# A graph attention layer: GpSimd's gathers spaced by an iota instead of waits for TensorE, and lookups issued ahead of kept-back products

## The chip, the cores and the metric

The kernel runs on one core of a Trainium2 chip. The metric is the device time of one execution in microseconds. Engines are named as the profile names them: PE is TensorE (its weight loads stand apart as PEld), DVE is VectorE, ACT is ScalarE, POOL is GpSimd and SP is SyncE.

## The reference

One layer of attention over the edges of a graph, with a residual and a layer norm. There are 12,500 nodes with 64 features, and 400,000 edges with 64 features, sorted by destination. Low-numbered nodes have by far the most edges.

```python
def _L0_gnn_ref(nfeats, efeats, W_ne, W_attn, b_attn, W_out, src, dst):
    h_src = nfeats[src]
    h_dst = nfeats[dst]
    z_att = jnp.concatenate([h_src, h_dst, efeats], axis=-1)
    e = jax.nn.leaky_relu(z_att @ W_attn + b_attn, negative_slope=0.01)[:, 0]
    m = jnp.concatenate([h_src, efeats], axis=-1) @ W_ne
    emax = jax.ops.segment_max(e, dst, num_segments=N)
    ex = jnp.exp(e - emax[dst])
    denom = jax.ops.segment_sum(ex, dst, num_segments=N)
    alpha = ex / denom[dst]
    z = jax.ops.segment_sum(alpha[:, None] * m, dst, num_segments=N)
    return jax.nn.relu(jnp.concatenate([nfeats, z], axis=-1) @ W_out)
x = _layernorm(x + _L0_gnn_ref(x, edge_attr_64, ...), axis=-1)
```

## The kernel before, in words

Edges are taken in 782 groups of 512 (128 partitions x 4). The groups go two ways.

**Gathered groups** (654 of them, from group 128 on) run in 42 chunks of mostly 16 groups, and a chunk in four tiles of four groups. For each group GpSimd issues four indirect DMAs (`gather`, L331). Each fetches one row of 65 numbers for each of 128 edges from a table in HBM into the tile `zx`, so a full chunk has 64 gathers. `zx` has eight buffers (`ZB`), two chunks' worth, and a buffer comes free when the products that read it are done. For a tile, VectorE makes the edges' scores (`scores`, L371 to L392) and, once the chunk's softmax is known, the weights `w` (L792). TensorE multiplies `zx` by `w` (`products`, L809, 16 matrix products a tile, each two matmul instructions in the profile), and VectorE adds the result into `acc` (L828).

**Dense groups** (the first 128, whose few destinations have very many edges) need no gather. TensorE looks up the sources' scores by a one-hot product (`look_turn` on ScalarE, `look_products` L442 on TensorE, `look_scores` L469 to L475 on VectorE). Later it counts, for each source node, the weights of its edges (`dense_counts`: one-hots `big` by ScalarE L483 and L484, weighted one-hots `lows` by VectorE L486, products L491, sum L509), and a product with all nodes' features (`node_products`, L568) ends each run of groups. Lookups run from chunk 1 on and counts from chunk 5 on, up to five groups in a chunk. They are woven into the chunks by hand.

**Order.** The engines' queues hold the program's order; nothing is reordered. A chunk issues the scores of its four tiles with pieces of dense work between them. After them comes the softmax, a chain of scans on VectorE with transposes of short rows on TensorE (L599 to a row, L602 back). It is cut into steps; after each of its first four parts `dense_work(n)`, n = 0 to 3, issues a piece of dense work. The products of a chunk's first two tiles (`NOW`) follow its softmax at once. Those of the third and fourth are kept back in `later`, and `some_products` issues them in the steps of the next chunk: a whole tile in step 0 and half a tile in the steps after it.

**The gathers' waits.** `BEHIND` lists places among a chunk's 64 gathers and for each a step of the chunk before: gather 28 waits for the last TensorE instruction issued in step 0, 33 for step 1, 42 for step 2, 48 for step 3, 56 and 61 for the products of the first and second tile. These waits hold from chunk 3 to the last of the full ones. `latest()` finds the instruction.

**In a step** the order is: lookup scores of the step before, sums, kept-back products, then the one-hot for a lookup (ScalarE, `look_turn`), the load of the row after it (SP, `look_row`), and the lookup's matmuls. The one-hot is made one lookup ahead.

Of the kernel before, what the change touches and what calls it, by code (L numbers as in the profile page):

```python
# [15 lines left out]
P = 128  # L16
# [9 lines left out]
S = 48  # L26
BG = 32
BIG = 6
LOWS = 6
SG = 4  # L30
BS = 16
DO = BS + 1
# [17 lines left out]
LATE = 8.0  # L50
NOW = 2
HALF = 2
BEHIND = ((28, 0), (33, 1), (42, 2), (48, 3), (56, "first"), (61, "second"))

BF16 = mybir.dt.bfloat16
I16 = mybir.dt.int16
# [3 lines left out]
def sorted_path(ctx, tc, x, dst, idx, edge, w_ne, w_attn, b_attn, w_out, out, flag):  # L60
# [6 lines left out]
    nc = tc.nc  # L67
# [11 lines left out]
    const = ctx.enter_context(tc.tile_pool(name="const", bufs=1))  # L79
# [33 lines left out]
    def nodes_of(g):  # L113
        return next(n for upto, n in NODS if g < upto)
# [7 lines left out]
    def kept_at(g):  # L122
        d = round_of(g)
        return g - begins[d] + d % 2 * BD
# [12 lines left out]
    for i in range(2):  # L137
# [20 lines left out]
    twice = const.tile([P, P], F32, name="twice")  # L158
    nc.vector.memset(twice, 0.0)

    low_rows = dram.tile([DG, P, T], BF16, name="low_rows")
    p_col = const.tile([P, 1], F32, name="p_col")
    nc.gpsimd.iota(p_col, pattern=[[0, 1]], base=0, channel_multiplier=-1,
                   allow_small_or_imprecise_dtypes=True)
    places = const.tile([P, NB * NOD], I16, name="places")
    nc.gpsimd.iota(places, pattern=[[1, NB * NOD]], base=0, channel_multiplier=0,
                   allow_small_or_imprecise_dtypes=True)
# [156 lines left out]
    def gather(g0, n, srcs, b0, plain, steps=()):  # L324

        zx = feats.tile([P, SG, T, EW + D], F32, name="zx")
        for g in range(n):
            for t in range(T):
                r = RP if g0 + g == NG - 1 else P
                at = srcs[0:r, g0 + g - b0, t:t + 1]  # L330
                row = nc.gpsimd.indirect_dma_start(  # L331
                    out=zx[0:r, g, t, 1:EW] if plain else zx[0:r, g, t, 0:EW], out_offset=None,
                    in_=x[:, :] if plain else table[:, :],
                    in_offset=bass.IndirectOffsetOnAxis(ap=at, axis=0))
                step = dict(BEHIND).get((g0 + g - b0) * T + t)
                if step is not None and step in steps:
                    tc.add_manual_dep(row.ins, steps[step].name,
                                      mybir.DependencyInfo(mybir.DependencyClass.Sync, mybir.DependencyReason.DATA),
                                      reason="gathers do not run ahead of the tensor engine")
        return zx  # L340
# [77 lines left out]
    def look_row(g):  # L418

        row = work.tile([P, P * T], BF16, name="low_of", bufs=1)  # L420
        nc.sync.dma_start(out=row, in_=low_rows[g:g + 1].rearrange("g p t -> g (p t)").to_broadcast([P, P * T]))
        return row

    def big():
        return work.tile([P, P, T], F32, name="big", bufs=BIG)

    def look_turn(row):

        hot = big()
        flat_ = hot.rearrange("l p t -> l (p t)")  # L430
        nc.scalar.activation(flat_, row, AF.Square, bias=p_col)
        nc.scalar.activation(flat_, flat_, AF.Relu, scale=-1.0, bias=1.0)
        return hot

    def spare():
        return psum.tile([P, SG, P], F32, name="pg", bufs=4).rearrange("p a b -> p (a b)")

    def look_products(hot, bank_):

        found = bank_[:, 0:T * NB].rearrange("p (t h) -> p t h", t=T)  # L440
        for t in range(T):
            nc.tensor.matmul(found[:, t, :], hot[:, :, t], s_src, start=True, stop=True)  # L442
        return found
# [33 lines left out]
    def dense_counts(g):  # L477
# [3 lines left out]
        for t in range(T):  # L481
            hi = big().rearrange("l p t -> l (p t)")[:, 0:wide]
            nc.scalar.activation(hi, places[:, 0:wide], AF.Square, bias=place[:, t, g:g + 1])  # L483
            nc.scalar.activation(hi, hi, AF.Relu, scale=-1.0, bias=1.0)  # L484
            lows.append(work.tile([P, P], F32, name="lows", bufs=LOWS))
            nc.vector.tensor_scalar(lows[t], count_, low[:, t, g:g + 1], kept[:, t, kept_at(g):kept_at(g) + 1],  # L486
# [15 lines left out]
    def dense_sum(g, to):  # L502

        _, vs = nc.values_load_multi_w_load_instructions(
            rel[0:1, g:g + 1], engines=(EngineType.DVE,), min_val=0, max_val=ND - nodes_of(g),
            skip_runtime_bounds_check_because=within)
        n = min(FIT, nodes_of(g))
        at = counts[:, :, ds(vs[0], n)]
        nc.vector.tensor_tensor(at, at, to.rearrange("p (h n) -> p h n", n=n), op=OP.add)  # L509
        for j in range(nodes_of(g) - FIT):  # L510
            at = counts[:, :, ds(vs[0] + FIT + j, 1)]
            nc.vector.tensor_tensor(at, at, more_nodes[j].unsqueeze(2), op=OP.add)
# [77 lines left out]
    def node_sum(g0, z):  # L590

        at = accd[0:D, ds(node_of(g0), ND)]
        nc.vector.tensor_tensor(at, at, z, op=OP.add)
# [222 lines left out]
    def add_in(g0, n, pg, b0, fac):  # L816
# [4 lines left out]
        for g in range(n):  # L821
            if g == 0 and fac is not None:
# [13 lines left out]
                   allow_small_or_imprecise_dtypes=True)  # L836
# [40 lines left out]
    with before:  # L877
# [23 lines left out]
        with tc.manual_schedule(engines={EngineType.DVE, EngineType.Pool, EngineType.Activation, EngineType.PE, EngineType.SP}):  # L901
# [30 lines left out]
            for g0 in range(0, NG, 3 * P):  # L932
                n = min(3 * P, NG - g0)
# [46 lines left out]
    def late_of(k):  # L980

        nc.vector.tensor_scalar(lates[:, k:k + 1], d0b[:, starts[k] + sizes[k] - 1:starts[k] + sizes[k]],
                                float(S - RING - zeroed[-1] * P), None, op0=OP.add)

    def raised():

        worst = tiny.tile([P, 4], F32, name="worst")
        bad = tiny.tile([P, 4], F32, name="bad")
        for i, (col, op) in enumerate(((fars, OP.max), (ups, OP.max), (lates, OP.max), (earlies, OP.min))):
            nc.vector.tensor_reduce(worst[:, i:i + 1], col, axis=AX.X, op=op)  # L990
        nc.vector.tensor_scalar(bad[:, 0:3], worst[:, 0:3], 0.0, None, op0=OP.is_gt)
        nc.vector.tensor_scalar(bad[:, 3:4], worst[:, 3:4], 0.0, None, op0=OP.is_lt)
        pbad = psum.tile([P, SG, P], F32, name="pg", bufs=4)[0:1, 0, 0:4]
        nc.tensor.matmul(pbad, ones_col, bad, start=True, stop=True)
        some = tiny.tile([1, 1], F32, name="some")
        nc.vector.tensor_reduce(some, pbad, axis=AX.X, op=OP.max)
        nc.vector.tensor_scalar(some, some, 1.0, None, op0=OP.min)
        nc.vector.tensor_copy(flag, some)
# [114 lines left out]
    with loop:  # L1113
# [9 lines left out]
        def add_up(most=SG * BG):  # L1123

            while sums and most:
                g0, n, pg, b0, fac = sums.pop(0)
                add_in(g0, n, pg, b0, fac)
                most -= 1
                k = starts.index(b0)
                if g0 + n == b0 + sizes[k]:  # L1130
                    done.extend(due[k])
# [16 lines left out]
        seen, dense_carry, resolved_at, at_rest = [], None, None, []  # L1148
# [3 lines left out]
        def alike(todo, ends_=chunk_ends):  # L1152
            n = 0
            while n < min(each_of(todo[0]) if todo else 0, len(todo)) and not (n and todo[n] in edges_) and not (n and todo[n] in ends_):
                n += 1
            return [todo.pop(0) for _ in range(n)]
# [12 lines left out]
        with tc.manual_schedule(engines={EngineType.PE, EngineType.DVE, EngineType.Activation, EngineType.SP, EngineType.Pool}):  # L1169
            ready, turns = {}, []  # L1170
            resting, batch_looks, batch_counts = None, [], []
# [12 lines left out]
            for k, G in enumerate(sizes):  # L1184
# [7 lines left out]
                if k:  # L1192
                    joined = resting
                    batch_looks = alike(looks, ())
# [16 lines left out]
                for i, (g0, n) in enumerate(lots[k]):  # L1211
# [5 lines left out]
                    if k and i == 0 and batch_looks:  # L1217
                        loads = look_loads(batch_looks[0], len(batch_looks))
                        rows_ahead = [look_row(batch_looks[0])]
# [90 lines left out]
                def dense_work(n):  # L1310

                    nonlocal opened, summed, resolved_at, node_z
                    if n == 1 and final:
                        late_of(k)
                        raised()
                    if n == 0 and node_z:
                        node_sum(*node_z)
                        if node_z[0] + chunk_sizes[-1] == DG:
                            resolved_at = k
                        opened = node_z = None  # L1320
                    if seen:
                        look_scores(*seen.pop(0))
                    if n > 1 and behind:
                        sums.append(behind.pop(0))
                    add_up(1)
                    if n in (0, 2, 3):
                        while open_counts:
                            dense_sum(*open_counts.pop(0))
                    for half in range(2 if n == 0 else 1):
                        if later:  # L1330
                            some_products()
                    if n + 1 < len(batch_looks):
                        if n:
                            turns.append(look_turn(rows_ahead.pop(0)))
                            if n + 2 < len(batch_looks):
                                rows_ahead.append(look_row(batch_looks[n + 2]))
                        seen.append((batch_looks[n + 1], look_products(turns.pop(0), spare())))
                    inner = batch_counts[len(early_counts):]
                    for g in inner[n - 4:][:1] if len(inner) >= 4 - n > 0 else ():
                        open_counts.append(dense_counts(g))  # L1340
# [511 lines left out]
```

## Time and profile before

| | |
|---|---|
| time, median of 3 runs | 4607.04 us (4581.74 to 4616.41) |
| the profiled execution's own time | 4585.0 us |
| its span, first to last instruction | 4583.3 us |
| mean granted TensorE clock | 0.675 |
| gathers | 2552 from the table, 64 from x |

The profile is that of one execution. A group of instructions is named by line, engine and operation, with output and inputs; `[idle before <-releaser]` gives the engine's idle time before an instruction and what ended it. "issue" means that the profile shows nothing that it waited for, and "remote" that a semaphore came at a time at which no instruction that adds to it ends. Ends of matmuls are modelled. The page's clock digits of the first fifth are 9 or 8 because the trace holds no clock record before 871 us.

### The profile page before, as it was taken

The numbers are of one execution on the slowest core, as the hardware profiler recorded it, in microseconds if no ns is written. First come the engines' busy times: TensorE is split into PE (matmuls) and PEld (weight loads), VectorE is DVE, ScalarE is ACT, GpSimd is POOL, SyncE is SP. The second block draws the span as 40 slices with busy tenths as digits, with TensorE's granted clock in tenths as the row PEclk, the third lists the DMA queues.
The fourth block names the chain that finished last, engine by engine and source line by source line (L and its number), as shares of the span: only waits on it lengthen the run. The fifth ranks groups of instructions, "written<-read, shape, count | busy, mean of one in ns | idle before, by whom it ended". The sixth has DMA issues, their size and how long they took to land. (4 is left out here: it accounts for less than half of the span.)

```text
span 4583.3 us, 38977 instructions
## 1 busy us (share of the span) xinstructions
PE 2480.8 (54%) x10315; PEld 2021.9 (44%) x10315; DVE 2158.0 (47%) x5618; ACT 1367.3 (30%) x2963; POOL 2478.9 (54%) x2644
## 2 busy tenths in 40 slices
PE   0144455565656667575666564455455565555544
PEld 0144445444545455454444444344343444444444
DVE  4444545454545545454535354444434454444346
ACT  0111223333323324242424232232323333323212
POOL 7566655555554555545464555555555545565543
PEclk9999999855556556566656566566566666666655
DMA  8222322232222222222222222222212222222111
GB/s 110 63 59 59 78 60 69 56 75 60 61 55 63 61 55 62 52 62 52 57 51 58 45 61 51 52 53 53 53 43 46 59 48 47 49 46 50 41 36 36
DMA packets 452951, 257.79 MB, mean 56 GB/s; under 512 B 266314, under 2 KB 410801, under 8 KB 452722
## 3 DMA queue, kind: packets, MB, share of 16 engines
q1 hardware_dynamic: 367036, 167.23, 14.4%
q0 software_dynamic: 83936, 87.27, 11.5%
q8 instruction: 88, 1.44, 0.1%
q14 instruction: 141, 1.16, 0.1%
q10 hardware_dynamic: 1750, 0.70, 0.1%
HBM read 248.17 MB, written 6.80 MB: 56 GB/s over the span
## 5 line engine op out<-in xcount | busy, mean ns | idle before, releaser
L331 POOL DMA_INDIRECT zx<-table,srcs x2552 | 2409.1, 944 | 2022.6 <-issue 823.1
L809 PE MATMUL pg<-w,zx 128*128 128x16 f32 (+9 forms) x5088 | 1063.0, 378 | 160.6 <-issue 118.1
L809 PEld LDWEIGHTS pg<-w,zx 128*128 128x128 f32 x5088 | 1047.8, 314 | 178.8 <-issue 118.9
L491 PE MATMUL pg<-big,lows 128*128 128x490 f32 (+3 forms) x1024 | 618.2, 758 | 733.3 <-DVE lows L486 256.0
L491 PEld LDWEIGHTS pg<-big,lows 128*128 128x128 f32 x1024 | 279.2, 293 | 1008.2 <-issue 731.1
L483 ACT ACTIVATE big<-places,place 128x490 f32<-128x490 int16 (+3 forms) x512 | 318.0, 621 | 581.5 <-remote 323.8
L442 PE MATMUL pg<-s_src,big 128*128 128x98 f32 x1024 | 282.0, 440 | 100.6 <-issue 100.6
L599 PE MATMUL lines<-ident,bnd 128*1 128x128 f32 x168 | 47.8, 384 | 500.4 <-ACT bnd L702 329.6
L442 PEld LDWEIGHTS pg<-s_src,big 128*128 128x128 f32 x1024 | 256.2, 328 | 101.7 <-issue 101.4
L471 DVE TENSOR_TENSOR pr<-pr,pg 128x392 f32<-128x392 f32 x128 | 72.0, 562 | 475.7 <-PE pg L442 283.8
L828 DVE TENSOR_TENSOR acc<-acc,pg 128x16 f32 (+9 forms) x654 | 121.7, 186 | 342.2 <-remote 235.1
L484 ACT ACTIVATE big<-big 128x490 f32<-128x490 f32 (+3 forms) x512 | 277.3, 542 | 16.3
L568 PE MATMUL pg<-xall,counts 128*128 128x256 f32 (+1 forms) x650 | 191.9, 447 | 120.9 <-issue 120.9
L599 PEld LDWEIGHTS lines<-ident,bnd 128*1 128x1 f32 x168 | 12.4, 96 | 522.3 <-ACT bnd L702 346.4
L486 DVE TENSOR_SCALAR lows<-fixed,low,kept 128x128 f32<-128x128 f32 x512 | 176.4, 403 | 105.9 <-remote 80.1
L376 DVE TENSOR_REDUCE soft<-pr 128x16 f32<-128x1024 f32 (+2 forms) x168 | 201.5, 1199 | 42.4 <-remote 24.4
L371 ACT ACTIVATE fixed<-wrow 128x144 f32<-128x144 f32 (+8 forms) x168 | 44.2, 263 | 593.8 <-DVE pr L469 171.3
L568 PEld LDWEIGHTS pg<-xall,counts 128*128 128x128 f32 (+1 forms) x650 | 146.5, 229 | 160.1 <-issue 137.4
L383 DVE TENSOR_TENSOR hot<-fixed,drel 128x576 bf16<-128x576 f32 (+8 forms) x168 | 106.8, 636 | 199.1 <-ACT fixed L371 183.9
L374 DVE TENSOR_TENSOR pr<-ze,lines 128x1024 f32<-128x1024 f32 (+2 forms) x168 | 198.6, 1182 | 2.1 <-DMA ze<-in_edge_dram 2.0
L509 DVE TENSOR_TENSOR counts<-counts,pg 128x490 f32 (+3 forms) x128 | 74.9, 585 | 250.5 <-remote 164.8
L372 ACT ACTIVATE zx<-ze 128x1024 f32<-128x1024 f32 (+2 forms) x168 | 174.0, 1036 | 5.6 <-issue 1.0
(308 smaller groups left out, 2743.9 us busy)
## 6 DMA issues: line engine op xcount, KB each, us to landing
ze<-in_edge_dram SPq DMA_DIRECT2D x157, 512.0 KB
zx<-table,srcs POOLq DMA_INDIRECT x2552
low_of<-low_rows SPq DMA_DIRECT2D x128, 128.0 KB
ep<-in_edge_dram SPq DMA_DIRECT2D x128, 128.0 KB
wrow<-wins SPq DMA_DIRECT2D x152, 96.0 KB
ed<-in_edge_dram SPq DMA_DIRECT2D x14, 640.0 KB
ed<-in_edge_dram SPq DMA_DIRECT2D x14, 384.0 KB
table<-xall SPq DMA_DIRECT2D x7, 455.0 KB
```

The source lines that it names most:

```text
L331: row = nc.gpsimd.indirect_dma_start(out=zx[0:r, g, t, 1:EW] if plain else zx[0:r, g, t, 0:EW], out_offset=None, in_=x[:, :] if plain else ...
L372: nc.scalar.activation(zx[0:r, 0:n, :, EW:EW + D], ze[0:r, 0:n], AF.Copy)
L374: nc.vector.tensor_tensor(pr[0:r, 0:n], ze[0:r, 0:n], w_edge[0:r].unsqueeze(1).to_broadcast([r, n, T, D]), op=OP.mult)
L376: nc.vector.tensor_reduce(ysum[0:r, 0:n], pr[0:r, 0:n], axis=AX.X, op=OP.add)
L442: nc.tensor.matmul(found[:, t, :], hot[:, :, t], s_src, start=True, stop=True)
L483: nc.scalar.activation(hi, places[:, 0:wide], AF.Square, bias=place[:, t, g:g + 1])
L484: nc.scalar.activation(hi, hi, AF.Relu, scale=-1.0, bias=1.0)
L486: nc.vector.tensor_scalar(lows[t], count_, low[:, t, g:g + 1], kept[:, t, kept_at(g):kept_at(g) + 1], op0=OP.is_equal, op1=OP.mult)
L491: nc.tensor.matmul(to, lows[t], highs[t], start=(t == 0), stop=(t == T - 1))
L568: nc.tensor.matmul(pairs[0:m * ND, 0:m * D], counts[:, h0:h0 + m, :].rearrange("l h n -> l (h n)"), xall[:, h0:h0 + m, 1:EW], start=(h0 == ...
L809: nc.tensor.matmul(pg[:, g, :], zx[:, g, t, 1:EW + D], w[:, g, t, :], start=(t == 0), stop=(t == T - 1)).ins
L828: nc.vector.tensor_tensor(ag, ag, pg[:, g, :], op=OP.add)
```

## The change

Four edits are made together. An iota on GpSimd fills 264 16-bit columns of a tile that nothing reads, behind every second gather. The list of the gathers' waits is empty. In a step, the lookup's matmuls, the next one-hot and the next row's load come ahead of the kept-back products. And the tile `lows` has five buffers instead of six.

```diff
-LOWS = 6
+LOWS = 5
+PACE = 264
...
-BEHIND = ((28, 0), (33, 1), (42, 2), (48, 3), (56, "first"), (61, "second"))
+BEHIND = ()
...
+    paced = const.tile([P, PACE], I16, name="paced")
...
                     in_offset=bass.IndirectOffsetOnAxis(ap=at, axis=0))
+                if t % 2 == 1:
+                    nc.gpsimd.iota(paced, pattern=[[1, PACE]], base=0, channel_multiplier=0,
+                                   allow_small_or_imprecise_dtypes=True)
                 step = dict(BEHIND).get((g0 + g - b0) * T + t)
...
                         while open_counts:
                             dense_sum(*open_counts.pop(0))
+                    if n + 1 < len(batch_looks):
+                        seen.append((batch_looks[n + 1], look_products(turns.pop(0), spare())))
+                        if n + 2 < len(batch_looks):
+                            turns.append(look_turn(rows_ahead.pop(0)))
+                            if n + 3 < len(batch_looks):
+                                rows_ahead.append(look_row(batch_looks[n + 3]))
                     for half in range(2 if n == 0 else 1):
                         if later:
                             some_products()
-                    if n + 1 < len(batch_looks):
-                        if n:
-                            turns.append(look_turn(rows_ahead.pop(0)))
-                            if n + 2 < len(batch_looks):
-                                rows_ahead.append(look_row(batch_looks[n + 2]))
-                        seen.append((batch_looks[n + 1], look_products(turns.pop(0), spare())))
```

## The prediction

> **What bounds the kernel now.** I read the page first: no engine is busy for much over half of the span, so the time lies in waits.
>
> ```profile
> span 4583.3 us, 38977 instructions
> PE 2480.8 (54%) x10315; PEld 2021.9 (44%) x10315; DVE 2158.0 (47%) x5618; ACT 1367.3 (30%) x2963; POOL 2478.9 (54%) x2644
> ```
>
> Next the timeline of VectorE. The reciprocal on L753 runs once in each of the 42 chunks and so marks them; these are the ends of chunks 0, 2, 4 and 38.
>
> ```profile
> 201.83 0.96 DVE L753 RECIPROCAL level<-soft 128x128 f32<-128x128 f32 x1
> ...
> 368.06 0.96 DVE L753 RECIPROCAL level<-soft 128x128 f32<-128x128 f32 x1
> ...
> 552.25 0.96 DVE L753 RECIPROCAL level<-soft 128x128 f32<-128x128 f32 x1
> ...
> 4385.08 0.96 DVE L753 RECIPROCAL level<-soft 128x128 f32<-128x128 f32 x1
> ```
>
> Chunks 1 and 2 took 83.1 us each, 3 and 4 took 92.1, and the 34 chunks from 5 to 38, which also count, (4385.1 - 552.3) / 34 = 112.7. They are 84% of the span, and the question is what fills them. GpSimd's timeline gives its pace:
>
> ```profile
> 1130.55 0.94 POOL L331 DMA_INDIRECT zx<-table,srcs  x1 [0.30 <-issue]
> 1131.80 0.94 POOL L331 DMA_INDIRECT zx<-table,srcs  x1 [0.30 <-issue]
> ...
> 1158.01 0.94 POOL L331 DMA_INDIRECT zx<-table,srcs  x1 [0.30 <-issue]
> ...
> 2175.14 0.94 POOL L331 DMA_INDIRECT zx<-table,srcs  x1 [0.30 <-issue]
> ```
>
> A gather takes 1.25 us with its gap, the 64 of a chunk 80 us, so in 112.7 us GpSimd pauses for 32.7. The last two rows end two runs of gathers, at 1159.0 and at 2176. The view by windows, for one chunk, compares a stretch full of gathers with the pause behind it:
>
> ```profile
> core 0: us, PE busy (x) PEld busy (x) DVE busy (x) ACT busy (x) POOL busy (x), PEclk, DMA share, GB/s
> 1120.60:1159.00 38.40, 14.38 (x38) 8.85 (x37) 15.26 (x39) 9.34 (x20) 29.22 (x31) 0.54 0.34 79
> 1159.00:1181.90 22.90, 13.50 (x52) 10.68 (x52) 8.91 (x21) 6.62 (x15) 0.00 (x0) 0.50 0.04 8
> ```
>
> TensorE starts 1.0 matmul per us while gathers run and 2.3 once they have stopped, at about the same granted clock. That alone could be demand. TensorE's timeline beside the second of those runs shows that it isn't:
>
> ```profile
> 2135.36 12.16 PE L568 MATMUL pg<-xall,counts 128*128 128x256 f32 x41
> ...
> 2153.47 0.58 PE L568 MATMUL pg<-xall,counts 128*128 128x256 f32 x1 [2.45 <-issue]
> 2156.27 0.58 PE L568 MATMUL pg<-xall,counts 128*128 128x256 f32 x1 [2.22 <-issue]
> ...
> 2175.17 0.18 PE L552 MATMUL pg<-wd,ep 128*128 128x10 f32 x1 [2.62 <-issue]
> ...
> 2182.17 2.11 PE L552 MATMUL pg<-wd,ep 128*128 128x10 f32 x10 [0.52 <-issue]
> ```
>
> 41 matmuls start at 0.30 us each, then one per 2.8 us, waiting for nothing that the profile names ("issue"), and only 6 us after the run's last gather they go at 0.21 again. So a long run of gathers holds TensorE back. Others feel it as waits that end when no instruction ends ("remote"). From the view of waits:
>
> ```profile
> POOL zx L331 <- PE pg L442: 740.8, 29, 44.4
> ...
> DVE pr L471 <- PE pg L442: 283.8, 57, 21.9
> ...
> DVE acc L828 <- remote: 235.1, 32, 14.8
> DVE pr L576 <- remote: 195.2, 6, 36.0
> ...
> DVE counts L509 <- remote: 164.8, 20, 19.6
> ...
> DVE pr L471 <- remote: 147.4, 16, 16.7
> ...
> POOL zx L331 <- remote: 127.1, 44, 5.2
> ...
> DVE lows L486 <- remote: 80.1, 16, 13.4
> ...
> DVE counts L512 <- remote: 49.9, 7, 17.6
> ```
>
> VectorE carries the chain of a chunk (scores, softmax, weights), and its "remote" waits on matmul results sum to 872.5 us. That is the **lag** on which the forecast rests.
>
> **The change part by part.**
>
> *The iota.* It stands behind every second of 2552 + 64 gathers: 1308 of them. The trace has a long and a short one on GpSimd:
>
> ```profile
> L331 POOL DMA_INDIRECT zx<-table,srcs x2552 | 2409.1, 944 | 2022.6 <-issue 823.1 <-PE pg L442 740.8 <-remote 127.1
> ...
> L166 POOL IOTA places<- 128x686 int16 x1 | 0.7, 699 | 0.0
> ...
> L163 POOL IOTA p_col<- 128x1 f32 x1 | 0.1, 127 | 0.0
> ```
>
> Between 1 and 686 columns an iota costs (699 - 127) / 685 = 0.835 ns a column, so 264 take 127 + 263 x 0.835 = 0.35 us. The pair of gathers grows from 2.50 to 2.85 us; it would stay at 2.50 if the iota lay in the 0.30 us gap, and reach 3.15 if it brought a gap of its own. I take 2.85, since the iotas of the front follow one another without idle time. A chunk's gathers then need 32 x 2.85 = 91.2 us (80 to 101), 453 us more over the program. In the 34 chunks that is below 112.7 and costs nothing by itself. In chunks 1 to 4 (350.4 us in all) GpSimd becomes the bound: 4 x 91.2 - 350.4 = **+14 us**.
>
> What it gives: the share of streaming time in which GpSimd makes no gather rises from 0.60 of 2.50 (24%) to 0.95 of 2.85 (33%). No row shows how the lag answers to that. The ends are nothing at all (a gather costs TensorE the same whenever it runs) and nearly all of 872.5 us. I take the lag as inverse to that share: 1 - 0.24 / 0.333 = 28%, **-244 us**.
>
> *The waits taken out.* The 740.8 us on L442 will not become gathers. Of the eight buffers of zx a chunk fills four; gather 32 reuses one whose products are kept back to step 0 of the chunk before, where gather 28 waited for that step's lookup. So the pause stays, four gathers later and under the name L809. GpSimd is no bound there: 0.
>
> *Lookups first.* In a step the lookup's matmuls stood behind the kept-back products. Timelines of TensorE and VectorE in one chunk:
>
> ```profile
> 1172.77 7.01 PE L809 MATMUL pg<-w,zx 128*128 128x20 f32 x32
> 1179.62 2.15 PE L442 MATMUL pg<-s_src,big 128*128 128x98 f32 x8
> 1181.70 0.37 PE L602 MATMUL lines<-ident,line 1*128 1x1 f32 x2
> ```
>
> ```profile
> 1181.80 0.56 DVE L471 TENSOR_TENSOR pr<-pr,pg 128x392 f32<-128x392 f32 x1 [7.74 <-PE pg L442]
> 1182.40 0.56 DVE L473 TENSOR_REDUCE picked<-pr 128x4 f32<-128x392 f32 x1
> 1182.99 0.17 DVE L475 TENSOR_TENSOR y_dense<-y_dense,picked 128x4 f32<-128x4 f32 x1
> 1183.08 0.36 DVE L717 SCALAR_TENSOR_TENSOR soft<-pen,lines,soft 128x128 f32<-128x128 f32 x1
> ```
>
> With the lookup first, L471 runs 7 us earlier, but L717 needs the transposes of L602, which stay behind both: the 7.74 us wait moves there, and only the 1.29 us of L471 to L475 leave the chain. In the 57 places of that wait: **-74 us**. ScalarE's next one-hot and SP's load of the row after it move with it and stay a step ahead of use: 0. The products end one lookup (2.15 us) later; gather 32 waits for them, on an engine with 21 us to spare.
>
> *LOWS 5.* The second, not the third, left matrix of a following count waits for the first product of the count before. TensorE has three matmuls of that count queued as cover: 0. Without the cover each of the 128 counts waits for one product, two matmuls of this row:
>
> ```profile
> L491 PE MATMUL pg<-big,lows 128*128 128x490 f32 (+3 forms) x1024 | 618.2, 758 | 733.3 <-DVE lows L486 256.0
> ```
>
> 128 x 2 x 0.758 = 194 us, which goes to the range.
>
> *Sum.* 4583.3 + 14 - 244 - 74 = 4279. The profiled execution was timed at 4585.0, 22 us under the median of 4607.0, so about **4303 us**, 6.6% faster; the 34 chunks would take some 103.4 us.
>
> **The rivals.**
>
> *GpSimd becomes the bound.* The lag may answer sharply, since TensorE needs little relief to leave the 2.8 us pace. Then the 34 chunks fall to the gathers' 91.2 us and some 3 us of pause: 552.3 + 14 + 34 x 94.2 + 198.2 = 3967, so 3991 us. For it: the jump from 0.30 to 2.8 us. Against it: at 2182, free of gathers for 5 us, TensorE was only just recovered, and an iota gives 0.35.
>
> *No relief.* If each gather takes a fixed piece of TensorE's time, pacing only spreads it: the lag stays, lookups first and chunks 1 to 4 remain, 4583 + 14 - 74, and LOWS may eat that: 4545 to 4640, near 4590.
>
> *Slower: the run ends later.* The lag drains only some 6 us after a run of gathers (2176 to 2182 above), and VectorE's wait in the first of the two runs ends in the same way, 5.4 us behind its end at 1159.0:
>
> ```profile
> 1164.39 0.41 DVE L486 TENSOR_SCALAR lows<-fixed,low,kept 128x128 f32<-128x128 f32 x1 [3.80 <-remote]
> ```
>
>  The run of tiles 0 and 1 now has 16 iotas in it, 16 x 0.35 = 5.6 us, and four more gathers, 5.0 us; its short pauses, 127.1 / 34 = 3.7 us, go. If an iota is no relief to TensorE, the counts between the third and fourth tile's scores, which sit out that run, finish 5.6 to 10.6 - 3.7 = 6.9 us later in 34 chunks: 190 to 235 us, less 74, plus 14, and up to 194 more where LOWS loses its cover: 4735 to 4974, likeliest near 4760. It decides once TensorE in such a stretch still starts no more than 1.0 matmul per us.
>
> *VectorE pays for the iota.* If VectorE stood still for each iota that it meets, 47% of 453 us, 213 us at most, would come on top of the forecast: 4516. The Trainium skill has such a rule (SBUF — State Buffer, "SBUF: two separate sides"): VectorE and GpSimd share a port pair that one of them holds for a whole instruction, though two-input VectorE work is blocked only by GpSimd work that reads SBUF; an iota reads nothing, so by that page only VectorE's two-port forms would wait. No run here shows it yet.
>
> **How the numbers follow.** Forecast 0.50, GpSimd bound 0.18, no relief 0.12, slower 0.17, VectorE pays 0.03. Faster by over 1%: 0.50 + 0.18 + 0.03 = 0.71; within 1%, which is about what the spread of 4581.7 to 4616.4 lets one tell: 0.12; slower: 0.17. The forecast's own range, by the bounds of iota and LOWS and half or double the relief, is 4060 to 4500. The range of all reaches from 3991 past "no relief" into the slower case and leaves out most of that: 3990 to 4720.
>
> **What would show it.** Right: 1308 iotas of about 0.35 us, GpSimd busy near 2930 us, its wait on L442 gone and one on L809 of some hundred us in its place; VectorE's "remote" waits near 630 us; over 1.2 matmuls per us in the gathers' stretches; chunks of 103 us. The forecast is wrong if those waits stay near 870 us or fall under 300, if GpSimd pauses less than 5 us a chunk, or if VectorE's own instructions grow longer.

## The result and the profile after

| | median | range |
|---|---|---|
| before | 4604.7 us | 4581.7 to 4616.4 |
| after | 4778.9 us | 4764.9 to 4791.9 |

The ratio is 1.040, with an interval of 1.035 to 1.046: 4% slower where 6.6% faster was forecast. The profiled execution took 4764.9 us, its span is 4763.2 us and its granted clock 0.636. That clock is lower than before (0.675), and TensorE's same 10315 matmuls are busy for 2548.4 us instead of 2480.8; the run with the iota alone, below, is faster than before at a clock of 0.659, so the clock doesn't order these times.

From the page of the kernel after, the busy times, the gathers and the iota:

```profile
span 4763.2 us, 40098 instructions
...
PE 2548.4 (54%) x10315; PEld 2079.9 (44%) x10315; DVE 2163.8 (45%) x5618; ACT 1375.3 (29%) x2963; POOL 2961.8 (62%) x3952
...
L333 POOL DMA_INDIRECT zx<-table,srcs x2552 | 2414.1, 946 | 1709.0 <-issue 1432.2
...
L338 POOL IOTA paced<- 128x264 int16 x1308 | 477.6, 365 | 15.2 <-remote 3.2
```

Lines of the code stand 2 to 5 higher than before (the gather L333, the lookup L447, the kept-back products L814, the sums L514 and L517). Apart from the iotas no engine has new work, and none is near full. GpSimd sits idle for 1709 us; some 600 of these are the short gaps from one gather to the next (they are 602.0 us in the same kernel's run further down in which GpSimd never pauses), so some 1100 us are pauses. The same marker as before, the reciprocal, at the ends of chunks 4 and 38 in VectorE's timeline:

```profile
538.25 0.96 DVE L758 RECIPROCAL level<-soft 128x128 f32<-128x128 f32 x1
...
4571.48 0.96 DVE L758 RECIPROCAL level<-soft 128x128 f32<-128x128 f32 x1
```

(4571.5 - 538.3) / 34 = 118.6 us a chunk, against 112.7: 34 x 5.9 = 201 us, the loss and a little more: chunks 1 to 4 take 27 us longer too, but the time up to chunk 0's reciprocal is 41 us shorter (161.1 against 201.8) and that behind chunk 38's 6 us. Where it went is in the view of waits:

```profile
POOL zx L333 <- issue: 1447.9, 2575, 36.4
...
DVE acc L833 <- remote: 262.0, 36, 19.5
...
DVE counts L514 <- remote: 210.8, 36, 10.2
...
DVE counts L517 <- remote: 193.1, 24, 16.4
DVE soft L722 <- PE lines L607: 183.5, 34, 6.2
...
DVE pr L581 <- remote: 131.1, 5, 28.5
DVE lows L491 <- remote: 117.4, 16, 25.1
DVE lows L491 <- PE pg L496: 117.0, 17, 23.4
DVE pr L476 <- remote: 107.9, 22, 10.1
```

The six "remote" rows of the forecast now sum to 1022.3 us instead of 872.5. They were to fall to some 630. Last, one run of gathers, from 1292.6 to 1336.1, and the pause behind it, by windows, and the timelines of TensorE and ScalarE from within that run:

```profile
1292.60:1336.10 43.50, 17.99 (x69) 15.38 (x69) 18.43 (x48) 13.27 (x28) 36.06 (x48) 0.54 0.33 78
1336.10:1363.60 27.50, 18.13 (x62) 13.86 (x63) 14.72 (x37) 10.55 (x22) 0.03 (x2) 0.50 0.10 13
```

```profile
1304.98 4.18 PE L496 MATMUL pg<-big,lows 128*128 128x294 f32 x8
1333.19 1.35 PE L496 MATMUL pg<-big,lows 128*128 128x294 f32 x2 [24.03 <-issue]
```

```profile
1332.11 0.54 ACT L488 ACTIVATE big<-places,place 128x294 f32<-128x294 int16 x1 [23.05 <-remote]
1332.69 0.45 ACT L489 ACTIVATE big<-big 128x294 f32<-128x294 f32 x1
```

The 48 instructions of GpSimd are 32 gathers and 16 iotas without a break. TensorE works for the first 17 us and then starts nothing for 24.03 us, until the run is nearly over. The product at 1333.19 reads a one-hot `big`, and ScalarE ends one at 1333.14, begun only after 23.05 us of waiting for a semaphore event that no instruction's end explains. By these times a completion that came late to ScalarE kept TensorE without work. The mean of 69 / 43.5 = 1.6 matmuls per us hides that standstill.

One thing is needed to read what follows. The kernels ran on several chips, and the kernel before itself took 4552 to 4605 us on some and 3336 to 3343 us on others. On the first, TensorE's completions come late beside gathers, as in the trace above; I call these **late chips**. On the others the trace has no such wait. The ratio is always to the kernel before on the same chip.

### The profile page after: what moved, and what is told of

It reads as the page before. It is cut to its first block, busy times and chain, and to the rows that moved or that the text cites. A ratio compares the mean times of both kernels' runs of the same rounds, so it can differ in the third digit from the quotient of the medians.

```text
span 4763.2 us, 40098 instructions
## 1 busy us (share of the span) xinstructions
PE 2548.4 (54%) x10315; PEld 2079.9 (44%) x10315; DVE 2163.8 (45%) x5618; ACT 1375.3 (29%) x2963; POOL 2961.8 (62%) x3952
## 5 line engine op out<-in xcount | busy, mean ns | idle before, releaser
L333 POOL DMA_INDIRECT zx<-table,srcs x2552 | 2414.1, 946 | 1709.0 <-issue 1432.2
L814 PE MATMUL pg<-w,zx 128*128 128x16 f32 (+9 forms) x5088 | 1095.6, 381 | 442.3 <-issue 334.4
L814 PEld LDWEIGHTS pg<-w,zx 128*128 128x128 f32 x5088 | 1086.0, 320 | 454.8 <-issue 333.2
L496 PE MATMUL pg<-big,lows 128*128 128x490 f32 (+3 forms) x1024 | 640.5, 788 | 817.0 <-DVE lows L491 376.4
L496 PEld LDWEIGHTS pg<-big,lows 128*128 128x128 f32 x1024 | 291.4, 304 | 1098.7 <-issue 847.8
L338 POOL IOTA paced<- 128x264 int16 x1308 | 477.6, 365 | 15.2 <-remote 3.2
L447 PE MATMUL pg<-s_src,big 128*128 128x98 f32 x1024 | 276.0, 435 | 47.8 <-issue 47.7
L447 PEld LDWEIGHTS pg<-s_src,big 128*128 128x128 f32 x1024 | 253.8, 327 | 56.7 <-issue 52.5
L514 DVE TENSOR_TENSOR counts<-counts,pg 128x490 f32 (+3 forms) x128 | 74.9, 586 | 302.3 <-remote 210.8
```

Source lines behind the costliest of these rows:

```text
L333: row = nc.gpsimd.indirect_dma_start(out=zx[0:r, g, t, 1:EW] if plain else zx[0:r, g, t, 0:EW], out_offset=None, in_=x[:, :] if plain else ...
L338: nc.gpsimd.iota(paced, pattern=[[1, PACE]], base=0, channel_multiplier=0, allow_small_or_imprecise_dtypes=True)
L496: nc.tensor.matmul(to, lows[t], highs[t], start=(t == 0), stop=(t == T - 1))
L814: nc.tensor.matmul(pg[:, g, :], zx[:, g, t, 1:EW + D], w[:, g, t, :], start=(t == 0), stop=(t == T - 1)).ins
```

## The experiments

Two theories stood against each other at first: that taking the waits out costs the time (W), and that the iotas do (I); later products (R) and the lost fifth buffer (L) came third. The first four kernels each make one part of the change alone.

**The waits alone.**

```diff
-BEHIND = ((28, 0), (33, 1), (42, 2), (48, 3), (56, "first"), (61, "second"))
+BEHIND = ()
```

> The kernel before with only the gathers' waits for TensorE taken out (no iota, six lows, products first). Theory W, the waits were the breaks in which TensorE caught up inside the softmax part of a chunk: slower by 3 to 6% (4740 to 4880 us), VectorE's waits marked remote well over the 983 us of before, runs of 32 gathers unbroken. Rival I, the iotas are the cost since they lengthen each run of gathers by 9% without helping TensorE: within 1% of before (4560 to 4650). Rival L, the fifth left-matrix buffer was the cover: within 1%.

Measured: 4825.5 us, 1.056 (1.050 to 1.063) of a kernel before of 4559.6. That is +266 us for the edit that the prediction had priced at nothing, more than the whole loss. The kernel's own trace is less clear-cut than theory W: VectorE's "remote" waits rise only from 983 to 1090 us, and a chunk's gathers come in runs of 32, 16 and 16 more often than in two of 32.

**The iota alone**, with the fifth buffer that makes room for its tile.

```diff
-LOWS = 6
+LOWS = 5
+                if t % 2 == 1:
+                    nc.gpsimd.iota(paced, ...)
```

> The kernel before with the iota behind every second gather, its waits kept, products first; five lows, since six do not fit beside the iota's tile. Theory W: within 1.5% of before (4540 to 4670). Rival I: slower by 3% or more (over 4740). If pacing does relieve TensorE, as the prediction had it: 4340 to 4480.

Measured: 4232.5 us, 0.931 (0.924 to 0.937). Theory I falls: the iota is worth -327 us where the waits stay. On the forecast's own yardstick the relief is as large as worked out: the six "remote" rows sum to 618.4 us, where the forecast had some 630. Its view of waits shows what the waits still do:

```profile
POOL zx L333 <- PE pg L447: 375.1, 26, 34.4
```

**Lookups first alone.** The last hunk of the diff, on the kernel before.

> The kernel before with only the lookups issued ahead of the kept-back products. The prediction's term: 74 us faster (4530). Theory W alone: between that and no change. Rival R, the later products and the transposes behind them lengthen the softmax chain and give buffers back later: slower by 1 to 3% (4650 to 4740).

Measured: 4576.0 us, 1.004 (1.000 to 1.007). The gain of 74 us is not there; if anything, 0.4% are lost. In its trace VectorE's waits for named TensorE instructions fall from 638 to 477 us, and its "remote" waits rise from 983 to 1102.

**Five buffers alone.** `LOWS = 5` on the kernel before.

> The kernel before with five lows buffers instead of six, nothing else. Theories W, I and R: within 1% (4560 to 4650). Rival L: slower by 2 to 4%, up to 194 us (4700 to 4800).

Measured: 4566.8 us, 1.002 (0.999 to 1.005). Nothing, as the prediction had it.

The next kernels start from the changed one, on another late chip (kernel before 4556.0 us).

**The waits written back.** The first diff above, reversed.

> The changed kernel with the six waits written back: iota, lookups ahead and five buffers stay. Theory W (the waits gave TensorE the breaks in which it catches up; taking them out is the whole loss): close to the run with the iota alone, 4232 us, give or take the 0.4% that lookups ahead showed by themselves, so 4180 to 4300, the chunks 5 to 38 near 103 us. Rival O (lookups ahead and the iota hurt each other, since the kept-back products now stand behind lookups): 4400 or more even with the waits back.

Measured: 4249.0 us, 0.932 (0.923 to 0.940). One list of six pairs turns 4% slower into 7% faster.

**The changed kernel without its iotas.**

> The changed kernel without its iotas: waits out, lookups ahead, five buffers. It prices the iota where no wait breaks the gathers. The prediction's own term (a relief of some 230 us, or the 327 us that the iota brought with the waits kept) holds without waits too: 4779 + 230 to 327 = 5010 to 5110 us. Theory W with breaks as the thing that counts (an iota of 0.365 us is no break): the relief is mostly lost, and the time is that of the run with the waits taken out alone, 4825 us, so 4790 to 4880.

Measured: 4838.3 us, 1.062 (1.056 to 1.068). So without the waits the iota is worth 59 us by the times, or 1.062 - 1.040 = 2.2% by the ratios (the changed kernel was timed on another chip), where it brings 327 us or 6.9% with them. On late chips, in us:

| | no iota | iota |
|---|---|---|
| waits kept | 4552 to 4605 | 4232, 4249 |
| waits out | 4826, 4838 | 4779 |

The two parts are not additive: 4560 + 266 - 327 would be 4499.

**Three iotas for one**, waits out.

```diff
-                    nc.gpsimd.iota(paced, ...)
+                    for _ in range(3):
+                        nc.gpsimd.iota(paced, ...)
```

> The changed kernel with three iotas in place of one behind every second gather, waits still out. A pair of gathers then takes about 2.72 + 2 x 0.43 = 3.6 us by the measured pair and iota, 32 pairs 115 us a chunk, and GpSimd becomes the bound. Theory P (what counts is the rate of gathers; spacing alone gives TensorE its time): the chunks 5 to 38 take 115 to 119 us, bound by GpSimd, 4560 to 4720 us in all, and DVE's remote waits fall below 900 us. Theory W (only a break of some us lets the late completions through): runs of 32 gathers are 115 instead of 87 us a chunk, TensorE is late all through them, 4850 us or more, remote waits at 1200 us or more.

Measured: 4790.4 us, 1.052 (1.046 to 1.058). The total lies between the two theories, and the profile decides for P. The longest of VectorE's waits, and the shares of the chain that ended last:

```profile
DVE soft L387 <- DMA zx<-table,srcs: 1746.4, 122, 23.1
```

```profile
POOL 63%; issue 16%; PE 14%; DVE 4%; DMA 2%; ACT 1%; DVEq 0%; POOLq 0%; ACTq 0%
```

No "remote" row of VectorE is left. It waits for gathers, and GpSimd is the bound, at 115.6 us a chunk. So at a pair of gathers per 3.56 us nothing is late, at one per 2.73 us much is, on the same kind of chip. The 4560 to 4720 fell short on the first chunks (453 us for chunks 1 to 4, at GpSimd's pace too) and the end.

**Pauses in place of the waits.** No semaphore: GpSimd itself spends some 3.3 us ahead of three gathers.

```diff
+PAUSES = ((28, 0), (42, 2), (56, "first"))
...
+                if dict(PAUSES).get((g0 + g - b0) * T + t) in steps:
+                    for _ in range(8):
+                        nc.gpsimd.iota(paced, ...)
```

> The changed kernel with eight more iotas (about 3.4 us of GpSimd's own time, no semaphore) ahead of gathers 28, 42 and 56 of a chunk, the three places at which the gathers broke off in the run with the iota alone; the waits stay out. Theory B (a break of some us is what TensorE needs, whoever makes it): most of the loss comes back, 4300 to 4500 us, GpSimd at about 97 us a chunk is not yet the bound. Theory M (the moment counts: the waits hold the gathers until TensorE has done a given product, and a break at GpSimd's own time comes at the wrong moment): 4700 to 4850 us, as the changed kernel.

Measured: 4055.9 us, 0.891 (0.886 to 0.896), below what either theory gave, and the best time here on a late chip: it beats the kernel before and the changed one. With the iotas behind the pairs, a break needs no product to wait for. The chunks take 98.1 us, and GpSimd needs 32 x 2.73 + 3 x 3.12 = 96.7 of them (eight iotas take 3.27 us, less 0.15 of a gap that they fill): it is the bound now.

**Two iotas; pauses alone; shorter pauses; short pauses often.** Four variants were to tell rate from break: two iotas behind every second gather; the pauses without the iotas behind the pairs; five instead of eight iotas in a pause; four iotas behind every eighth gather.

> The changed kernel with two iotas in place of one behind every second gather, waits still out. With one, a pair of gathers takes 2.73 us and DVE waits 1288 us on late completions; with three, 3.56 us and none at all, and GpSimd is the bound at 115.6 us a chunk. Two give a pair of about 3.14 us, 101 us a chunk. Theory T (a threshold: below some rate of gathers nothing is late): no lateness, bound by GpSimd at 101 to 103 us a chunk, some 4790 x 3.14 / 3.56 = 4230, so 4200 to 4300 us. Theory G (gradual: lateness falls with the rate): remote waits of DVE about half, 500 to 700 us, 4350 to 4600 us.

> The changed kernel without the iotas behind every second gather, and with eight iotas (about 3.4 us) ahead of gathers 28, 42 and 56 of a chunk; waits out. It asks whether the breaks do all the work. GpSimd needs 32 x 2.50 + 3 x 3.4 = 90 us a chunk, 8 us less than with both. Theory B (breaks do it all): no slower than with both, 3950 to 4100 us. Rival (the spacing within a run counts as much, as the runs with and without the iota, waits kept, say: 7%): 4250 to 4450 us.

> The changed kernel with an iota behind every second gather and five more (about 2.1 us) ahead of gathers 28, 42 and 56; waits out. With eight, the chunks 5 to 38 take 98.1 us and GpSimd needs 97 to 98 of them: if GpSimd was the bound there and the shorter break still lets the late completions through, 94 to 95 us a chunk and 3930 to 4000 us. Rival (the break has to be as long as the backlog needs, and 2.1 us is too short): 4100 to 4350 us, remote waits of DVE above those of the run with eight (976 us).

> The changed kernel with four iotas (about 1.7 us) behind every eighth gather in place of one behind every second; waits out. The same 32 iotas a chunk as in the changed kernel, gathered into eight breaks: GpSimd needs 32 x 2.50 + 8 x 1.7 = 93 to 94 us a chunk. Theory B (time in one piece counts): most of the loss comes back, 3980 to 4250 us. Rival (only the mean rate counts; it is lower than the changed kernel's by 7%): 4500 to 4750 us.

They met a chip on which the kernel before takes 3336.3 us. Measured there, in this order: 4237.0 us (1.270, 1.268 to 1.272), 3676.0 (1.102, 1.100 to 1.104), 3859.7 (1.157, 1.155 to 1.159) and 3868.1 (1.159, 1.158 to 1.161). That the first lies where theory T had it is no confirmation: nothing was late in any of them, so they could not tell the theories apart. All are simply as slow as GpSimd, with 102.1, 89.3, 93.5 and 93.0 us a chunk.

**The changed kernel, and the waits alone, where nothing is late.** The same two kernels as above, beside two of the four, on one more chip (kernel before 3343.0 us).

> The changed kernel itself, once more. The last four kernels met a chip on which the kernel before takes 3336 us and TensorE's completions come on time; on the chips of the other runs it takes 4556 to 4605 us and they come late. Theory C (lateness belongs to the chip; where it is absent the stream of gathers on GpSimd is the bound and an iota costs its own time): if the kernel before takes some 3340 us here, the changed kernel takes 1308 x (2.73 - 2.50) = 306 us more, 3640 to 3710 us, 9 to 11% slower; if it takes some 4560 us here, 4730 to 4800 us, 4% slower, as first measured. Rival (the fast chip makes up for it in another way, so that what counts is the change's own gain): the predicted 0.93 to 0.94 of the kernel before on a chip that is not late.

> The kernel before without its six waits, once more, for the same reason. Theory C: where completions come on time the waits wait for nothing, so 3300 to 3345 us beside 3336 us; where they come late, 1.05 to 1.07 of the kernel before, as first measured (1.056). Rival (the waits keep something else apart, such as buffers): slower by 5% on either chip.

Measured: the changed kernel 3642.0 us, 1.089 (1.088 to 1.091); the waits alone 3342.5 us, 1.000 (0.999 to 1.001). Theory C holds with its numbers. The waits are worth nothing where nothing is late, and the iotas cost 1308 x 0.23 = 301 us, measured 299. The rows of the kept-back products in the changed kernel, on the late chip and on this one, and this one's chain that ended last:

```profile
L814 PE MATMUL pg<-w,zx 128*128 128x16 f32 (+9 forms) x5088 | 1095.6, 381 | 442.3 <-issue 334.4
```

```profile
L814 PE MATMUL pg<-w,zx 128*128 128x16 f32 (+9 forms) x5088 | 1051.4, 379 | 36.7 <-DVE w L797 36.5
...
POOL 59%; issue 13%; PE 13%; DVE 8%; DMA 3%; ACT 2%; DVEq 0%; POOLq 0%; ACTq 0%; SPq 0%
```

A matmul takes the same time on both. What is gone is the idle time before it for which the profile has no name.

**The pauses alone and two iotas again**, in the same company.

> Waits out, no iota behind the pairs, eight iotas (3.4 us) ahead of gathers 28, 42 and 56. On the chip that is not late it took 3676 us, bound by GpSimd at 89 us a chunk. On a chip that is late: theory B (breaks do all the work) 3680 to 4100 us; rival (the spacing within a run counts as much) 4250 to 4450 us. With both spacing and breaks it took 4056 us on such a chip.

> Two iotas behind every second gather, waits out. On the chip that is not late 4237 us, bound by GpSimd at 102 us a chunk. On a chip that is late: theory T (a threshold: below some rate nothing is late, as with three iotas, where DVE had no wait on a late completion) the same 4230 to 4260 us; theory G (gradual) 4350 to 4600 us with 500 to 700 us of such waits.

Measured: 3683.5 us (1.102, 1.100 to 1.104) and 4245.6 us (1.270, 1.268 to 1.272). The same as on the first chip of this kind; again no test of rate against break.

**The pauses alone, on a late chip** (kernel before 4551.6 us).

> Waits out, no iota behind the pairs, eight iotas (3.4 us) ahead of gathers 28, 42 and 56, a third time: on the two chips where nothing comes late it took 3676 and 3684 us, bound by GpSimd. If the kernel before takes some 3340 us here, the same again. If it takes some 4560 us: theory B (breaks alone do the work) 3680 to 4100 us, at most the 4056 us of spacing and breaks together; rival (the spacing within a run of gathers counts as much) 4250 to 4450 us.

Measured: 4753.5 us, 1.042 (1.034 to 1.050), above what either theory gave. Pauses alone do no more than iotas alone, and they don't replace the waits at whose places they stand (1.042 against 1.000). TensorE's timeline beside a run of gathers with such a pause in it (at 1543.4), and GpSimd's:

```profile
1510.40 3.58 PE L498 MATMUL pg<-big,lows 128*128 128x392 f32 x8
1556.36 3.89 PE L498 MATMUL pg<-big,lows 128*128 128x392 f32 x6 [42.38 <-ACT big L491]
```

```profile
1542.49 0.94 POOL L338 DMA_INDIRECT zx<-table,srcs  x1 [0.30 <-issue]
1543.44 3.27 POOL L336 IOTA paced<- 128x264 int16 x8
1546.87 0.94 POOL L338 DMA_INDIRECT zx<-table,srcs  x1 [0.15 <-issue]
```

TensorE stands still for 42.38 us, through the pause and until 4.8 us after the run's last gather (1551.5). It waits for ScalarE's one-hot, and ScalarE for a completion. The trace's events on TensorE's semaphore show it: of six instructions that add to it and end between 1508.6 and 1514.0, the first is reported at 1545.1, within the pause, and the other five between 1555.1 and 1555.3, behind the run.

Such events can be counted (some that coincide are recorded as one). Call an event late if no TensorE instruction that adds to the semaphore ends within 0.15 us of it, and a pause any stretch of over 1 us between two gathers. In chunks 5 to 38:

| kernel | pauses, their time | late events | of these while gathers stream | per us of streaming | per us of pause |
|---|---|---|---|---|---|
| before | 142, 1170 us | 488 | 25% | 0.05 | 0.31 |
| waits out | 95, 1399 us | 469 | 25% | 0.04 | 0.25 |
| waits out, pauses alone | 138, 1367 us | 358 | 15% | 0.02 | 0.22 |
| iota alone | 97, 583 us | 533 | 59% | 0.11 | 0.37 |
| changed kernel | 74, 1116 us | 581 | 56% | 0.11 | 0.23 |
| pauses and iotas | 105, 413 us | 430 | 52% | 0.08 | 0.50 |

With three iotas for one there are 10 late events, and in the changed kernel on a chip where nothing is late none. So held completions come out in pauses, whoever makes them, and between gathers at 2.73 us a pair some two to four times as often as at 2.50. Where gathers follow at 2.50 us a pair, three rests of 3.27 us a chunk are too little; with the iotas behind the pairs as well they were enough. Why the waits, without iotas, do better than such rests isn't shown: a wait lasts until its product is done, a rest 3.27 us, and no run separates moment from length.

**The same rest in three long pauses.** Fourteen iotas in a pause, none behind the pairs, GpSimd's time per chunk as in the best run.

> Waits out, no iota behind the pairs, and fourteen iotas (14 x 0.416 = 5.8 us) in place of eight ahead of gathers 28, 42 and 56. GpSimd needs 32 x 2.50 + 3 x 5.8 = 97.4 us a chunk, the same as in the run with an iota behind each pair and breaks of 3.4 us (32 x 2.73 + 3 x 3.3 = 97.4). On a chip where completions come late (kernel before near 4560 us): theory N (only GpSimd's mean rate over a chunk counts) the same 4056 us, 4020 to 4120; theory D (the breaks must be spread: within a run of gathers at 2.50 us a pair nothing comes through, and only the iota behind each pair lets single completions out) 4250 to 4650 us. Where nothing is late (before near 3340 us): bound by GpSimd either way, 3676 + 34 x 7.5 = 3930, so 3900 to 3990 us, and it doesn't tell them apart.

Measured on a chip where nothing is late (kernel before 3342.6 us): 3952.8 us, 1.183 (1.181 to 1.185), 96.7 us a chunk, as GpSimd's time demands. Whether the mean rate or the spread of the rest decides on a late chip stays open.

## Why the prediction was wrong

**The step that failed is "the waits taken out: 0".** It argued that the pause stays, four gathers later, and that GpSimd is no bound. Both are true: from chunk 5 on GpSimd's long pause stands ahead of gather 32 (26 us in the median; before, 23 us ahead of gather 28), and it pauses for some 1100 us in all. But only this one pause was looked at. The waits also broke the second half of a chunk's gathers, at 33, 42, 48, 56 and 61, into pieces of mostly 5 to 15; the other run, of 31 or more gathers, stayed whole with them too. Those short breaks let held completions through: in the kernel before, 241 late events fall into its 108 pauses of up to 10 us. With the waits out 142 pauses become 95, 57 of them short, with 219 late events (74 and 32, with 97, in the changed kernel, whose runs are nearly all of 32); TensorE's standstills of over 10 us in chunks 5 to 38 grow from 579 to 903 us in all (816); and the edit costs 266 us. That the edit costs this is shown; that it does so because completions are held for longer with fewer breaks is argued from these counts, not measured. Writing the waits back undoes the loss; so do GpSimd's own pauses at three of their places, but only with the iotas kept. Where no completion is late, taking the waits out costs nothing.

**The iota's relief (-244 us) was a right mechanism with the wrong partner.** With the waits kept it was -327 us, more than forecast; without them -47 to -59 by the times (1.6 to 2.2% by the ratios). The sum added it to the waits' removal as if the two were independent. Much of the smaller gain has no term in the sum: the time up to chunk 0's reciprocal, for which the forecast had no change, is 199 to 200 us without iotas and 161.1 with them, waits out in all three. And the yardstick was poor. With pauses and iotas together VectorE's "remote" waits, 976 us in all rows, are what they were before (983), in a kernel 11% faster.

**The iota's price** came out lower than worked out. An iota takes 0.365 us against the 0.35 worked out, but it uses up half of the gap between two gathers, so that the pair grows from 2.50 to 2.73 us, not to 2.85. GpSimd's timeline in the kernel after:

```profile
1303.47 0.95 POOL L333 DMA_INDIRECT zx<-table,srcs  x1 [0.16 <-issue]
1304.73 0.95 POOL L333 DMA_INDIRECT zx<-table,srcs  x1 [0.31 <-issue]
1305.68 0.37 POOL L338 IOTA paced<- 128x264 int16 x1
1306.21 0.95 POOL L333 DMA_INDIRECT zx<-table,srcs  x1 [0.16 <-issue]
```

Chunks 1 to 4 took 538.3 - 161.1 = 377.2 us by the marker (chunk 0 ends at 161.1) instead of 350.4: +27, forecast +14. The nearness is chance, for the reason given fails: at 2.73 us a pair four chunks of gathers need 349.6 us, no more than the 350.4 of before, and the same chunks take 365 and 375 us in the two kernels with the waits out and no iota.

**Lookups first (-74 us)** gave nothing measurable. The wait moved to the transposes as foretold (the row on L722, 183.5 us in 34 places). The saving of 1.29 us a place did not reach the end: in the run with lookups first alone, VectorE's waits for TensorE by name fall by 161 us and its "remote" ones rise by 119, so that it waits for late completions in other places instead.

**LOWS 5: 0** held in the kernel before. In the changed kernel 17 places now wait 117.0 us for the product of L496 (row above); there it was not tried alone.

**The signs named.** Iota, GpSimd's busy time (2961.8 us, forecast 2930) and the vanished wait on the lookup came as said. The wait that was to appear on L809 did not: GpSimd's long waits end on "issue". The lag rose instead of falling. The matmul rate of 1.6 per us in the run above meets the forecast's sign of over 1.2 in a kernel that is slower: a mean over a run was a bad sign.

**The rivals.** "Slower: the run ends later" gave near 4760 us, and 4779 came. That nearness is luck. It counted the iotas as what lengthens a run and the vanished short pauses as a gain of 3.7 us a run; the runs show the reverse, since without iotas it is slower still (4838) and taking out the waits is the whole cost. Its condition, at most 1.0 matmul per us, did not hold in the run above. "GpSimd becomes the bound" came true in other kernels: with three iotas, with pauses, and wherever nothing is late. "VectorE pays" is refuted by VectorE's own durations, before and after:

```profile
L374 DVE TENSOR_TENSOR pr<-ze,lines 128x1024 f32<-128x1024 f32 (+2 forms) x168 | 198.6, 1182 | 2.1 <-DMA ze<-in_edge_dram 2.0
```

```profile
L379 DVE TENSOR_TENSOR pr<-ze,lines 128x1024 f32<-128x1024 f32 (+2 forms) x168 | 198.6, 1182 | 2.0 <-DMA ze<-in_edge_dram 1.9
```

That is what the Trainium skill (SBUF — State Buffer, "SBUF: two separate sides") lets one expect of an instruction with two inputs beside an iota, which reads nothing. All of VectorE's instructions together took 2163.8 us instead of 2158.0, 5.8 us more where this rival had up to 213.

**Not settled.** What holds TensorE's completions back on some chips. The gathers' own packets take the same time with the waits out, whether late or not. The row of their queue on the late chip and on the other:

```profile
q0 software_dynamic: 83936, 87.27, 9.7%
```

```profile
q0 software_dynamic: 83936, 87.27, 13.7%
```

9.7% of 4829.9 us is 468 us an engine, 13.7% of 3334.9 is 457. So the transfers are not what is slower. Nor do the runs say whether lateness belongs to a chip for good: each chip held to it for all runs made together, and the one met twice (for the changed kernel again, and for the long pauses) was on time both times.

## What to carry to other kernels

A wait that delays an engine with time to spare can still be doing work, as the break in which another engine's held completions come through: before you take it out, look at what happens on the other engines at its places, and price it together with the other edits that act on the same lag, not as one term of a sum. Judge a stream by the sum of the standstills beside it, not by its mean rate, nor by the longest one: in chunks 5 to 38 TensorE's longest is 38.7 us in the kernel before and 30.5 in the slower changed one, while those of over 10 us sum to 579 and 816 us, and to 380 with the iota alone. And run the kernel before on more than one chip: here the best pacing on one kind (0.89; not itself run on the other) belongs to a family that cost 9 to 27% on the other, where the plain kernel is already at GpSimd's pace (without its waits, which cost nothing there, 79.8 us a chunk, and 64 gathers of 1.25 us are 80).

## What the runs showed of the hardware

I had not expected that one program takes 4560 us on some chips and 3340 us on others, while its instructions last as long (in the changed kernel the matmuls of the kept-back products 381 and 379 ns). On late chips TensorE's completions are held while gathers stream: with the waits out it stood still for 42.38 us at a pair per 2.50 us, even across a pause of 3.27 us, and for 24.03 us at a pair per 2.73 us, each time until ScalarE's next one-hot, for which ScalarE had itself waited for a late completion; at a pair per 3.56 us VectorE had no late completion to wait for. Held completions come out at 0.22 to 0.50 per us in pauses, at 0.08 to 0.11 between gathers with an iota behind each pair, and at 0.02 to 0.05 without.
